# The last pair of a state-space block: decays and gates recorded ahead of the previous pair's outputs

## The chip, the core and the metric

The kernel runs on one core of a Trainium2 chip, in one launch. The metric is the time of the launch on the device in microseconds (us), the median of several runs; lower is better. Five engines of the core work side by side, each through its own queue in the order of that queue: TensorE (PE in the profile, with its weight loads as PEld), VectorE (DVE), ScalarE (ACT), GpSimd (POOL) and SyncE (SP), which here only issues DMAs. They wait for each other by semaphores.

## The reference

Two pre-norm layers act on x, 4 sequences of 256 positions with 512 features. Cut to its frame:

```python
x = x + attn0(layernorm(x))    # 1: gated linear attention, 32 heads, chunks of 128
x = x + ffn0(layernorm(x))     # 2: top-8 router over 64 experts, a bias mix
x = x + attn1(layernorm(x))    # 3: state space: conv, decays, gate, group norm, out_proj
x = x + ffn1(layernorm(x))     # 4: top-16 of 64 low-rank adapters
```

The change is in block 3, the state space, as it hands over to block 4. What block 3 computes for one head, with chunks of 128 positions:

```python
hs, B, C = split(silu(conv4(x @ W_x)))           # causal convolution of 4 taps
L        = exp(segsum(dt * A))                   # the decays, 128 x 128, lower triangle
Y        = (C @ B.T * L) @ (hs * dt) + off_chunk + D * hs
g        = Y * silu(x @ W_gate)
out      = rmsnorm_by_group(g) * norm_w @ W_out
```

Block 4 takes a layernorm of the result, scores 64 adapters, keeps 16, softmaxes them into gates, and computes `((x @ A) * gates) @ B`.

## The kernel before

**Tiling.** x stays on the chip as eight tiles of 128 positions by 512 features (`k.x[0..7]`). Tiles 0 to 3 are half 0 (sequences 0 and 1), tiles 4 to 7 half 1. The normalized input of a half is held transposed, split into two parts `xs_hi` and `xs_lo`. Each weight is split likewise by `split` (L138 on ACT makes the high part, L141 on POOL the low part), and each product is three matmuls of 128x512: high by high, low by high, high by low. A projection (`proj`, L200) is 12 such matmuls.

**Block 3** goes by pairs of 128-channel tiles: 8 groups, 4 pairs in a group, 2 halves, so 64 pairs, in the list `pairs`. The last four are, as (group, pair, half): (7,2,0), (7,3,0), (7,2,1), (7,3,1). I write U for (7,3,0), the last pair of half 0; V for (7,2,1); and Z for (7,3,1), the last pair of all. Every pair goes through these steps, each named by a letter; a digit is the channel tile (0, 1) or, for O, the output tile (0 to 3):

- I `inputs`: projection ps_x, then the convolution (L712 on ACT, three times L714 on DVE) and Silu (L1115 on ACT).
- X `sums`: a DMA brings running sums into gb, and m is formed from them (L293 on DVE and POOL, L295 on POOL).
- D `decays`: two Exp on ACT (L1115), then m times C.B, 128x1536, on DVE (L753).
- G `gate`: projection ps_g, then Silu on ACT.
- T `turn`: four transposes into ps_t (L775), then xd (L777) and xe (L786) on DVE. xe lies in the buffer with the tag "xn", of which there is one; the normalization of block 4 takes the same buffer for its first and fourth tile.
- M `mixer`: 24 small matmuls into ps_y (L800); then xs on DVE (L810), times the gate on POOL (L814), yh on ACT (L818), yl on DVE (L819); the square on ACT (L826) and its sum on POOL (L828).
- O `output`: six matmuls into ps_o (L854), added to acc on DVE (L860). At the last pair of a group also the scale r (L834 on PE, L839 on DVE, L840 on POOL), and L863 on DVE adds the scaled acc to the four x tiles of the half.
- B, the shared projection of a group, does nothing for the last pair. W splits one more weight, if one is due.
- P and E `pump`: one step of side work from `k.side`. E may also run a step that needs another activation table.

**Staging.** One round i of the loop in `run` takes three neighbouring pairs: O is of `before` (pair i-1), T and M are of `p` (pair i), and I, G, X, D are of `after` (pair i+1). The order inside a round is a string of letters, written out by hand: STEP3, or SIDE3 if `k.side` is not empty as the round begins. PSUM has eight banks by tags of two: "x", "y", "o" and "g"; ps_o has the tag "o", so a ps_o waits until the acc step two outputs before it has been done.

The scheduler keeps the recorded order as a priority and may move instructions of one engine past each other.

**Handing over.** When O3 of U is recorded, half 0 is ready, and `prepare4(0)` of block 4 goes into `k.side`. Its steps: wr (the router weight, put into the tag "xd" and then split: L962 on ACT, L963 on POOL, into the buffer that acc of half 0 leaves); the moments (L86, L88 on DVE, rstd by L90 and L91 on POOL) and the first centred tiles xn (L99); four steps of transposes ps_xn (L107) with the parts xs_hi (L124, ACT) and xs_lo (L125, DVE); the scores ps_lg; their top 16 on DVE (L976 to L996); then eight projections ps_h; in their course the gates are transposed (L999), copied (L1001) and sent by DMA to DRAM and back, spread (L1047). The same for half 1 follows when O3 of Z is recorded. Block 4 proper multiplies ps_h by the gates (L1056), splits it (L1061, L1062) and multiplies by B (L1077).

The round that the change touches is the one with p = V, before = U, after = Z. In the kernel before, `k.side` is empty as it begins, so its order is STEP3. The rounds after it use SIDE3.

Of the kernel before, what the change touches and what calls it, by code (L numbers as in the profile page):

```python
# [18 lines left out]
P = 128  # L19
# [13 lines left out]
STEP1 = "K S0 W T S1 S2 W G0 G1 K C K P U A0 K W P A1 T P P Q0 N0 W W N1 Q1 T T W K D F".split()  # L33
SIDE1 = "S0 W G0 T P K C W W P P W S1 K G1 S2 U P A0 N0 A1 P Q0 T W T F W N1 K Q1 T T D W W".split()
STEP3 = "W T0 T1 B I0 W M0 M1 X0 X1 I1 O0 G0 W W O1 W W P O2 W W G1 P W O3 D0 D1 W W".split()
SIDE3 = "T0 T1 I0 I1 M0 M1 P B X0 X1 P P O0 W O1 G0 G1 W W P O2 O3 W P W P D0 D1 E E".split()


# [615 lines left out]
def state_space(k, tc, io):  # L654
# [65 lines left out]
    def group(p):  # L720

        g, half = p.g, p.half
        bc = [
            k.wk.tile([P, FREE], F32, tag="y", name=f"bc_{g}_{half}_{n}", bufs=4) for n in range(2)
        ]
        for n, first in enumerate((BS, CS)):
            conv(proj(k, tc, chunk(p.w.bc(), n), half, f"bc_{g}_{half}_{n}"), bc[n], first + g)
        s = own.only.tile([P, 3, 2, P], F32, tag="cb", name=f"cb_{g}_{half}", bufs=2)
        for b in range(2):
            ps = k.psum.tile([P, 3, P], F32, tag="x", name=f"ps_cb_{g}_{half}_{b}")  # L730
            for n, (zs, zl) in enumerate(((0, 0), (1, 1), (0, 1))):
                fs, fl = (2 * b + zs) * P, (2 * b + zl) * P
                nc.tensor.matmul(
                    ps[:, n, :], bc[0][:, fs:fs + P], bc[1][:, fl:fl + P],
                    start=True, stop=True,
                )
            nc.scalar.copy(s[:, :, b, :], ps)
        cbs[g, half] = s

    def sums(p, n):  # L740
        hs = slice(2 * (p.ch + n), 2 * (p.ch + n) + 2)
        p.e[n] = exponents(
            k, tc, cum[p.half][:, hs, :], start[p.half][:, :, hs], f"{p.name}_{n}", 2
        )

    def decays(p, n):


        m, across = p.e.pop(n)
        k.act(m[:, 2], across, AF.Exp)  # L750
        k.act(m[:, 0:2], m[:, 0:2], AF.Exp)
        mh = m.rearrange("p z (h b) l -> p z h (b l)", h=2)
        made = nc.vector.tensor_tensor(  # L753
            mh, mh, cbs[p.g, p.half].rearrange("p z b l -> p z (b l)").unsqueeze(2)
            .to_broadcast([P, 3, 2, 2 * P]), ALU.mult,
        )
        p.m.append(m)
        p.due.append(made)

    def inputs(p, n):  # L760
        xs = k.wk.tile([P, FREE], F32, tag="a", name=f"xs_{p.name}_{n}", bufs=4)
        conv(proj(k, tc, chunk(p.w.x(), n), p.half, f"x_{p.name}_{n}"), xs, p.ch + n)
        p.xs.append(xs)

    def gate(p, n):
        sg = k.wk.tile([P, FREE], F32, tag="sg", name=f"sg_{p.name}_{n}", bufs=4)
        k.act(sg, proj(k, tc, chunk(p.w.g(), n), p.half, f"g_{p.name}_{n}", "g"), AF.Silu)
        p.sg.append(sg)

    def turn(p, n):  # L770

        nm, ch, xs = f"{p.name}_{n}", p.ch + n, p.xs[n]
        ps = k.psum.tile([P, HT, P], F32, tag="y", name=f"ps_t_{nm}")
        for t in range(HT):
            nc.tensor.transpose(ps[:, t, :], xs[:, t * P:t * P + P], k.ident)  # L775
        xd = k.wk.tile([P, HT, 2, D], F32, tag="xd", name=f"xd_{nm}")
        made = nc.vector.tensor_tensor(  # L777
            xd, ps.rearrange("p t (h d) -> p t h d", h=2),
            dt[p.half][:, :, 2 * ch:2 * ch + 2].unsqueeze(3)
            .to_broadcast([P, HT, 2, D]), ALU.mult,  # L780
        )
        p.xd.append(xd)
        p.due.append(made)
        if n == 0:
            p.xe = k.wk.tile([P, 2, 2, 2, D], F32, tag="xn", name=f"xe_{p.name}", bufs=1)
        made = nc.vector.tensor_tensor(  # L786
            p.xe[:, n], ps.rearrange("p (b z) (h d) -> p b z h d", b=2, h=2)[:, :, 0],
            start[p.half][:, 2, 2 * ch:2 * ch + 2, :].rearrange("p h b -> p b h").unsqueeze(3)
            .to_broadcast([P, 2, 2, D]), ALU.mult,
        )  # L790
        p.due.append(made)
# [50 lines left out]
    def output(p, t):  # L842
        if p.cp == 0 and t == 0:
            acc[p.g, p.half] = k.wk.tile([P, HT, HID], F32, tag="big", name=f"acc_{p.name}")
        if p.cp == NC // 2 - 1 and t == 0:
            scale(p)
        ps = k.psum.tile([P, HID], F32, tag="o", name=f"ps_o3_{p.name}_{t}")
        at = slice(t * P, t * P + P)
        i = 0
        for n in range(2):  # L850
            yh, yl = p.y[n]
            wh, wl = p.w.o()
            for y, w in ((yh, wh), (yh, wl), (yl, wh)):
                nc.tensor.matmul(ps, y[:, at], w[:, n, :], start=(i == 0), stop=(i == 5))  # L854
                i += 1
        a = acc[p.g, p.half][:, t, :]
        if p.cp == 0:
            nc.scalar.copy(a, ps)
        else:
            nc.vector.tensor_tensor(a, a, ps, ALU.add)  # L860
        if p.cp == NC // 2 - 1:
            xt = k.x[HT * p.half + t]
            nc.vector.scalar_tensor_tensor(xt, a, p.r[:, t:t + 1], xt, ALU.mult, ALU.add)  # L863
# [3 lines left out]
    pairs = []  # L867
# [21 lines left out]
    def run(done):  # L889


        with tc.tile_pool(name="s3", bufs=1, reuse_waits="tile") as own.only:
            for i in range(-1, len(pairs) + 1):
                k.bank = BANK3
                before, p, after = (
                    pairs[j] if 0 <= j < len(pairs) else None for j in (i - 1, i, i + 1)
                )
                if i + 2 < len(pairs):
                    k.weights.due = pairs[i + 2].w.g.n
                else:  # L900
                    k.weights.due = len(k.weights.all) - 1
                if after is not None and after.half not in ready:
                    k.pump(1000, True)

                def shared():
                    if after.cp == 0:
                        group(after)

                def put(t):
                    output(before, t)  # L910
                    if t == HT - 1 and all(one.half != before.half for one in pairs[i:]):
                        done(before.half)

                step = dict(
                    B=shared, I=lambda n: inputs(after, n), G=lambda n: gate(after, n),
                    X=lambda n: sums(after, n), D=lambda n: decays(after, n), T=lambda n: turn(p, n), M=lambda n: mixer(p, n),
                    O=put, W=k.weights.step, P=k.pump, E=lambda: k.pump(1, True),
                )
                for one in SIDE3 if k.side else STEP3:
                    who = {"T": p, "M": p, "O": before, "P": k, "E": k, "W": k}.get(one[0], after)  # L920
                    if who is not None and (i >= 0 or not AHEAD or one[0] not in "IG"):
                        step[one[0]](*(int(n) for n in one[1:]))
# [325 lines left out]
```

## Time and profile before

| what | value |
|---|---|
| median of 3 runs | 2592.67 us (2592.57 to 2594.05) |
| the profiled execution, time | 2597.62 us |
| the profiled execution, span of the core | 2595.9 us |
| mean granted TensorE clock | 0.983 |
| PE busy | 2468.8 us, 95% |
| DVE busy | 2082.8 us, 80% |
| ACT busy | 1531.7 us, 59% |
| POOL busy | 1528.2 us, 59% |
| DMA | 206.18 MB, mean 79 GB/s |

The profile is of one execution; its span and its time differ by 1.7 us of launch, and its time is 4.95 us above the median. "PE 128*128 128x512" is a matmul with a 128x128 weight over 512 columns. In a timeline a row has the start, the duration, the engine, the line and what it writes and reads; brackets give the idle time before it and what ended it. In a table of windows, PEclk is the clock that TensorE was granted in that stretch, 1.00 being full speed. Places in the trace are given in us from the start of the span.

### The profile page before, as it was taken

The page shows a single profiled execution, that of the slowest core. Times are in us where ns is not written, and L with a number is a line of the kernel's source. Part 1 is how long each engine was busy: PE and PEld are TensorE (multiplying, and loading weights), DVE is VectorE, ACT ScalarE, POOL GpSimd, SP SyncE. Part 2 cuts the span into 40 slices and gives each one's busy share as a digit, 9 for nine tenths or more (in the row PEclk, how much of TensorE's full clock was granted, in tenths as well). Part 3 has the DMA queues.
Part 4 walks back from the last instruction along what each step waited for, and adds up shares of the span by engine and source line. Part 5 has one row for each costly group of instructions (what it writes and reads, how often), then busy time and mean ns, then how long its engine had stood idle before and what let it go on. Part 6 is the DMA issues. An engine that isn't in the chain of part 4 may idle for free.

```text
span 2595.9 us, 35580 instructions
## 1 busy us (share of the span) xinstructions
PE 2468.8 (95%) x13488; PEld 1998.4 (77%) x13488; DVE 2082.8 (80%) x2694; ACT 1531.7 (59%) x2109; POOL 1528.2 (59%) x996
## 2 busy tenths in 40 slices
PE   7899999999999888989999999999999999999889
PEld 6777787888777676768878788788787887887667
DVE  6777777778888767797997888888888888879963
ACT  3665565666665545565765756666656657657531
POOL 4554445456655545586774864856766756747840
PEclk9999999999999988999999999999999999999989
DMA  3321111212221222242322222322323223323321
GB/s 106 82 66 49 54 52 57 66 57 90 90 86 56 86 73 69 80 120 74 98 90 66 84 88 82 98 73 78 102 65 98 82 74 93 96 63 100 94 73 67
DMA packets 82891, 206.18 MB, mean 79 GB/s; under 512 B 8672, under 2 KB 10592, under 8 KB 82720
## 3 DMA queue, kind: packets, MB, share of 16 engines
q1 hardware_dynamic: 82720, 203.90, 25.8%
q8 instruction: 107, 1.75, 0.3%
q14 instruction: 64, 0.52, 0.1%
HBM read 200.86 MB, written 3.01 MB: 79 GB/s over the span
## 4 chain that ended last, share of the span: by engine, by line
PE 59%; DVE 25%; ACT 5%; POOL 5%; issue 4%; DMA 2%; SPq 0%; POOLq 0%; ACTq 0%; DVEq 0%
PE ps_g L200 12%; PE ps_o L854 8%; PE ps_x L200 6%; PE ps_o L458 6%; PE ps_q L200 6%; DVE conv L714 5%; DVE m L753 5%; PE ps_y L800 3%; PE ps_y L411 3%; PE ps_sc L399 2%; DVE x L863 2%; PE ps_bc L200 2%; DVE m L293 2%; PE ps_h L200 2%; PE ps_o L1077 2%
## 5 line engine op out<-in xcount | busy, mean ns | idle before, releaser
L200 PE MATMUL ps_g<-xs_hi,wg_h 128*128 128x512 f32 x768 | 309.2, 403 | 18.5 <-ACT wg_h L138 7.3
L200 PE MATMUL ps_g<-xs_lo,wg_h 128*128 128x512 f32 x768 | 305.5, 398 | 0.0
L200 PE MATMUL ps_g<-xs_hi,wg_l 128*128 128x512 f32 x768 | 304.1, 397 | 1.1 <-POOL wg_l L141 1.1
L753 DVE TENSOR_TENSOR m<-m,cb 128x1536 f32<-128x1536 f32 x128 | 264.9, 2081 | 47.5 <-ACT m L1115 43.2
L714 DVE SCALAR_TENSOR_TENSOR conv<-ps_x,cw,conv 128x510 f32<-128x510 f32 (+2 forms) x384 | 270.7, 737 | 17.7 <-ACT conv L712 14.4
L1112 ACT ACT_TABLE_LOAD x193 | 247.6, 1283 | 3.9 <-PEq L1236 0.8
L141 POOL TENSOR_TENSOR wo_l<-raw_wo,wo_h 128x1024 fp32r<-128x1024 f32 x60 | 154.8, 2580 | 136.1 <-ACT wo_h L138 136.1
L1115 ACT ACTIVATE xs<-conv,cb 128x512 f32<-128x512 f32 x128 | 91.6, 723 | 239.9 <-DVE conv L714 236.8
L293 POOL TENSOR_TENSOR m<-gb,start 128x512 f32<-128x512 f32 x128 | 152.4, 1194 | 136.1 <-PE ps_y L800 107.8
L814 POOL TENSOR_TENSOR xs<-xs,sg 128x512 f32<-128x512 f32 x128 | 201.2, 1572 | 43.1 <-DVE xs L810 42.5
L854 PE MATMUL ps_o<-wo_h,yh 128*128 128x512 f32 x512 | 213.0, 416 | 9.8 <-DVE acc L860 6.9
L295 POOL TENSOR_SCALAR_AFFINE_SELECT m<-m 128x1024 f32<-128x1024 f32 x160 | 216.0, 1350 | 1.5 <-DVE m L293 1.4
L200 PE MATMUL ps_x<-xs_hi,wx_h 128*128 128x512 f32 x512 | 206.4, 403 | 7.8 <-DVE conv L714 7.8
L854 PE MATMUL ps_o<-wo_h,yl 128*128 128x512 f32 x512 | 200.5, 402 | 6.4 <-DVE yl L819 6.3
L200 PE MATMUL ps_x<-xs_lo,wx_h 128*128 128x512 f32 x512 | 204.9, 400 | 0.0
L200 PE MATMUL ps_x<-xs_hi,wx_l 128*128 128x512 f32 x512 | 203.6, 398 | 0.0
L854 PE MATMUL ps_o<-wo_l,yh 128*128 128x512 f32 x512 | 203.1, 397 | 0.0
L828 POOL TENSOR_TENSOR sqs<-sqs,sq 128x512 f32<-128x512 f32 x112 | 173.0, 1545 | 48.6 <-ACT sq L826 48.1
L141 POOL TENSOR_TENSOR wx_l<-raw_wx,wx_h 128x1024 fp32r<-128x1024 f32 x38 | 97.7, 2571 | 176.1 <-DVE conv L714 115.8
L141 POOL TENSOR_TENSOR wg_l<-raw_wg,wg_h 128x1024 fp32r<-128x1024 f32 x60 | 158.9, 2648 | 61.0 <-ACT wg_h L138 58.9
L200 PEld LDWEIGHTS ps_g<-xs_hi,wg_h 128*128 128x128 f32 x768 | 144.8, 189 | 61.0 <-issue 17.1
L800 PE MATMUL ps_y<-m,xd 128*64 128x128 f32 x2048 | 177.2, 279 | 14.3 <-DVE m L753 13.6
(281 smaller groups left out, 6963.9 us busy)
## 6 DMA issues: line engine op xcount, KB each, us to landing
gb<-cum SPq DMA_DIRECT2D x160, 512.0 KB
raw_wx<-in_L_attn_in_x_dram SPq DMA_DIRECT2D x38, 512.0 KB
raw_wg<-in_L_attn_in_gate_dram SPq DMA_DIRECT2D x38, 512.0 KB
raw_wo<-n_L_attn_out_proj_w_dram SPq DMA_DIRECT2D x38, 512.0 KB
raw_wq<-in_L_attn_Wq_dram SPq DMA_DIRECT2D x22, 512.0 KB
raw_wg<-in_L_attn_Wg_dram SPq DMA_DIRECT2D x22, 512.0 KB
raw_wo<-in_L_attn_Wo_dram SPq DMA_DIRECT2D x22, 512.0 KB
raw_wkv<-in_L_kv_dram SPq DMA_DIRECT2D x11, 512.0 KB
```

The source lines that it names most:

```text
L141: nc.gpsimd.tensor_tensor(lo, w, hi.bitcast(F32), ALU.subtract)
L200: tc.nc.tensor.matmul(ps, a[:, c, :], b[:, c, :], start=(c == 0 and n == 0), stop=(c == KC - 1 and n == 2))
L293: engine.tensor_tensor(m[:, blk], gb[:, min(blk, 1)], last(at, P), ALU.add)
L295: nc.gpsimd.affine_select(out=causal, in_=causal, compare_op=ALU.is_ge, fill=GONE, base=0, pattern=[[0, 8], [1, P]], channel_multiplier=-1,)
L458: nc.tensor.matmul(ps, y[:, 2 * h + b, :], w[:, h, :], start=(i == 0), stop=(i == 5))
L714: nc.vector.scalar_tensor_tensor(acc[:, :, j:], ps[:, :, :SEQ - j], cw[:, ch, TAPS - 1 - j:TAPS - j], acc[:, :, j:], ALU.mult, ALU.add,)
L753: made = nc.vector.tensor_tensor(mh, mh, cbs[p.g, p.half].rearrange("p z b l -> p z (b l)").unsqueeze(2) .to_broadcast([P, 3, 2, 2 * P]), ...
L800: one = nc.tensor.matmul(ps_y[h * D:h * D + D, 2 * b + z, :], p.xe[:, n, b, h, :] if blk == 2 else xd[:, 2 * b + zs, h, :], m[:, blk, 2 * ...
L814: nc.gpsimd.tensor_tensor(xs, xs, p.sg[n], ALU.mult)
L828: nc.gpsimd.tensor_tensor(total, total, sq, ALU.add)
L854: nc.tensor.matmul(ps, y[:, at], w[:, n, :], start=(i == 0), stop=(i == 5))
L1112: load = nc.scalar.preload_act_table_set(table)
```

## The change

For the one round whose `after` is the last pair, a third order is used:

```diff
 STEP3 = "W T0 T1 B I0 W M0 M1 X0 X1 I1 O0 G0 W W O1 W W P O2 W W G1 P W O3 D0 D1 W W".split()
+LAST3 = "T0 T1 I0 I1 X0 X1 M0 M1 G0 G1 W D0 D1 W O0 O1 P W O2 O3 P W P P E P E".split()
 SIDE3 = "T0 T1 I0 I1 M0 M1 P B X0 X1 P P O0 W O1 G0 G1 W W P O2 O3 W P W P D0 D1 E E".split()
...
-                for one in SIDE3 if k.side else STEP3:
+                for one in LAST3 if after is pairs[-1] else SIDE3 if k.side else STEP3:
```

Against STEP3, both gates of Z (G0, G1) and both decays of Z (D0, D1, with the products of L753) are recorded ahead of all four outputs of U. I1 is recorded ahead of M0, as are X0 and X1. Behind O3, where STEP3 has D0 D1, there are six pumps: wr, the moments and the four transposes of half 0 of block 4 are thus recorded in this round, ahead of T, M and the outputs of the next one, which were ahead of them. There are four W in place of eleven. No instruction is added or removed in number on DVE, ACT, POOL, SP or PE.

## The prediction, made before the changed kernel had run

> **What bounds the kernel now.** I read the page first, for the engine that sets the time:
>
> ```profile
> PE 2468.8 (95%) x13488; PEld 1998.4 (77%) x13488; DVE 2082.8 (80%) x2694; ACT 1531.7 (59%) x2109; POOL 1528.2 (59%) x996
> PEclk9999999999999988999999999999999999999989
> PE 59%; DVE 25%; ACT 5%; POOL 5%; issue 4%; DMA 2%; SPq 0%; POOLq 0%; ACTq 0%; DVEq 0%
> ```
>
> The first line is busy time, the last the chain that ended last. PE is busy for 95% of the span, so nothing is won but where PE waits or is slowed; one of the few slices below 9 in PEclk is the last but one. So I read the table of windows from where the change begins to the end (columns: window, length, PE, PEld, DVE, ACT, POOL busy, PEclk, DMA share, GB/s):
>
> ```profile
> 2436.00:2456.00 20.00, 18.00 (x122) 14.57 (x120) 17.39 (x25) 11.17 (x16) 18.34 (x12) 1.00 0.26 79
> 2456.00:2470.00 14.00, 5.24 (x51) 4.07 (x50) 14.00 (x16) 2.44 (x3) 10.87 (x9) 0.76 0.29 86
> 2470.00:2485.00 15.00, 13.34 (x55) 9.95 (x55) 13.37 (x19) 7.34 (x12) 14.87 (x12) 0.89 0.27 76
> 2485.00:2512.00 27.00, 27.00 (x128) 21.73 (x127) 13.07 (x49) 7.95 (x13) 9.10 (x11) 1.00 0.14 41
> 2512.00:2526.00 14.00, 9.27 (x30) 6.73 (x29) 7.06 (x11) 4.54 (x9) 0.00 (x0) 0.63 0.35 105
> 2526.00:2592.00 66.00, 66.00 (x292) 53.56 (x290) 27.47 (x62) 9.79 (x16) 2.39 (x1) 1.00 0.21 72
> ```
>
> There are two weak places: 2452 to 2474, and 2512 to 2526. From 2526 PE is never idle, so a gain ahead of it reaches the end whole. In the first place DVE is busy for 14.00 of 14: it is the engine to follow there. Then the timeline of PE, the rows with idle time:
>
> ```profile
> 2455.04 0.50 PE L854 MATMUL ps_o<-wo_h,yh 128*128 128x512 f32 x1 [2.00 <-ACT yh L818]
> 2461.68 0.69 PE L800 MATMUL ps_y<-m,xd 128*64 128x128 f32 x4 [5.46 <-DVE m L753]
> 2465.51 0.44 PE L800 MATMUL ps_y<-m,xd 128*64 128x128 f32 x4 [1.01 <-DVE m L753]
> 2470.44 0.66 PE L107 MATMUL ps_xn<-ident,xn 128*128 128x128 f32 x4 [2.74 <-DVE xn L99]
> 2514.04 0.66 PE L107 MATMUL ps_xn<-ident,xn 128*128 128x128 f32 x4 [1.02 <-DVE xs_lo L125]
> 2517.30 0.76 PE L200 MATMUL ps_lg<-xs_hi,wr_parts 128*128 128x512 f32 x1 [2.60 <-DVE xs_lo L125]
> 2520.89 0.80 PE L200 MATMUL ps_lg<-xs_lo,wr_parts 128*128 128x512 f32 x1 [1.12 <-DVE xs_lo L125]
> ```
>
> With two small gaps (0.54, 0.67) PE waits for 17.2 us. It also runs at half clock: matmuls follow each other at 0.43 us instead of 0.23 after several of these gaps. Priced by the number of matmuls, that loses 1.4 us at 2461.7, 1.9 at 2470.4 to 2474.4 and 3.9 at 2514 to 2525.7, in all 7.2. So 24.4 us are lost here, 15.8 in the first place and 8.6 in the second (4.74 idle, 3.9 clock). More than 24 us cannot be won.
>
> **The change part by part.** In number nothing is added on any engine; all of the change is order. The built queues are the same up to the end of ps_y of V, 2439.65 us. From there PE does g of Z (24 matmuls), the rest of o_U0 and o_U1, ps_t of Z, o_U2 and o_U3, all of o_V, the four ps_xn of half 0, and only then ps_y of Z, the scores, and the ps_h with o_Z between them. Before, ps_y of Z stood ahead of every ps_xn.
>
> Part 1, gates and decays earlier. The g of Z end at 2445.3 by 0.23 us a matmul, so ACT has the last Silu at 2448.3 (2449.4 before), and after one table load (1.28) and its Exps at 2452.6 the second m (2454.3 before). DVE can run the two L753 at 2451.1 and 2454.7 instead of 2457.98 and 2462.06, ahead of the four L863, instead of behind. I take 3.0 us for each:
>
> ```profile
> L753 DVE TENSOR_TENSOR m<-m,cb x6: 2119/3006/3842, 2408.5 to 2462.1; 128x1536 f32<-128x1536 f32 x6
> ```
>
> (duration: shortest, median, longest.) The wait of 5.46 us for m thus goes, and m is early by 20 us where it is now used. But the two products now stand ahead of what PE needs: acc of o_U2, whose PSUM bank the o of V wait for, and yl of V. PE waits 0.85 us for r ahead of ps_t (behind yl of V, at 2449.0), 2.3 for acc behind the first product (to 2454.7), 2.7 for yl behind the second (to 2458.6), then 1.2 in two waits for acc. PE is through o_V at 2466.5.
>
> Part 2, six pumps early. The four L863 (mean 0.87, so 3.5 us) end at 2463.3. ACT's L962 follows them, as wr's parts take acc's buffer, and behind it in ACT's queue two casts of wa (1.04 each). On POOL L963 and two L141 (2.4 each) are queued ahead of the three L91 that give rstd: 2465.2, 2467.6, adds 2468.2, 2470.6, and rstd at 2471.2. In the kernel before, two of the three L91 were done at 2468.9. The first xn is ready at 2471.8: PE waits 5.3 us for it, where it waited 2.74. This is the new wait, and it takes the place of the old 5.46. In the chain xn, ps_xn, xs_hi, xs_lo three more gaps follow, 1.2, 1.6 and 0.8: xs_hi of the second tile is queued on ACT behind a cast of raw_wb, whose DMA leaves after the second L141, and the fourth xn shares its buffer with xe. ps_y of Z begins at 2478.1. The DMA of wr passes ahead of three raw_wa on SP; those wa are used 10 us later, so I cost that at nothing, and 1.0 us (one cast, as above) if that cover fails.
>
> The sum of gaps is 0.85 + 2.3 + 2.7 + 1.2 + 5.3 + 1.2 + 1.6 + 0.8 = 15.95 us. For the half clock I take one loss of 1.9 (as at 2470.4) after 2.7, one after 5.3, and 1.5 in the short gaps behind it: 5.3. The first place thus costs 21.2 instead of 15.8: worse by 5.4.
>
> [...] The row: after 2.00 us of idle (2455.04) the matmuls still came at 0.23, after 2.74 (2470.44) at 0.43. [...]
>
> Part 3, the end. The outputs of Z now stand between the ps_h, which are work for PE while the top 16 of half 0 are found. The gates leave earlier: L999 at 2502.9 instead of 2508.3, gT at 2503.5 instead of 2509.6, and with the 6.25 us from gT to the first L1056 and 1.85 from one to the next, as before, the first gates come at 2509.8 and 2511.65. So half 1 is normalized with 12 o-matmuls beside it and PE waits 1.1 us in place of 4.74, at full clock: 7.5 of the 8.6 are won.
>
> Sum: 5.4 - 7.5 = **-2.1 us**. The profiled run took 2597.62, 4.95 above the median; the same difference from the median gives 2590.6.
>
> The bounds of what is unknown: both L753 at 2.12, -1.8; no half clock after 2.7, -1.9; no gap in the tail, -1.1; yl at its median 0.92 instead of 1.65, -0.7: together -7.6. Upwards: L753 at 3.84, +1.7; one L141 at 3.87 (as at 2459.88), +1.5; half clock for another four us behind the 5.3, +1.9: together +3.0. I take the middle values, because DVE and POOL are as full here as in the rows they come from.
>
> **The rivals.** *Cheap middle, faster.* The low ends come together: DVE is ahead, as the decays no longer collide with the moments. For it speaks that L753 has a mean of 2.08 over the whole kernel; against it, that POOL is busy for 18.34 of 20 us where the products now go, and the products on either side took 3.84 and 3.56. At -7.6: 2585.1; if the 2.3 gap and the loss of clock after the 5.3 go too, -11.8, 2580.9.
>
> *Late gates, slower.* In the new queue of DVE the first L1056, which waits for a DMA, is ahead of the last moments and xn of half 1, and on ACT the hid_h of the second gate is ahead of the copy that empties a PSUM bank for ps_h. By my times that copy ends at 2513.6 and PE needs the bank at 2514.1: 0.5 us of room. From a gT later than 2504 on, PE waits, the clock falls, and the 8.6 of the tail stay. For it speaks that gT hangs on L996, whose chain the first place delays; against it, that o_Z gives PE 48 matmuls (11 us) to bridge. At 5.4 + 0 to + 1.7 (L753 at 3.84): between +5.4 and +7.1, 2599.0; with 1.0 for the cast as well, 2600.8.
>
> That the change moves nothing is excluded by the built queues.
>
> **How the numbers follow.** Forecast .46, cheap middle .30, late gates .24. A measurement of this kernel can tell about 0.2%, 5.2 us, from no change. The forecast's own range, 2585.1 to 2595.7, is mostly within that: .32 same, .12 faster, .02 slower. The cheap middle is .30 faster; late gates .23 slower, .01 same. Faster .42, same .33, slower .25. The range runs from 2581 to 2600.
>
> **What would show it.** In the timeline of PE: no wait for m L753 ahead of ps_y; a wait of about 5 us for xn L99, 2.3 and 2.7 us ahead of L854; PEclk of 1.00 from 2512 on. On DVE both L753 ahead of the L863. gT earlier by 6 us. It is wrong if the ps_xn are not late, or if ps_h waits for a raw4 copy behind L1061.

## The result, and the profile after

The changed kernel is slower: 2600.55 us against 2594.41 us (medians of 22 runs each), a ratio of 1.0022 with an interval of 1.0015 to 1.0030, which is 5.7 us (3.9 to 7.8). A second comparison gave 1.0014 (1.0005 to 1.0023). The kernel before, compared with itself in the same way, gave 1.0005 (0.9995 to 1.0014): differences under 0.1% are not read as differences below. The forecast was -2.1 us.

The page of the changed kernel (profiled run 2600.39 us, span 2598.7 us):

```profile
PE 2471.4 (95%) x13488; PEld 1999.9 (77%) x13488; DVE 2081.2 (80%) x2694; ACT 1530.7 (59%) x2109; POOL 1530.3 (59%) x996
PEclk9999999999999988999999999999999999999889
PE 60%; DVE 24%; ACT 6%; POOL 4%; issue 4%; DMA 2%; SPq 0%; POOLq 0%; ACTq 0%; DVEq 0%
```

PE has 2.6 us more busy time with the same number of matmuls, and one slice more of PEclk, the last but two, is below 9: the clock, not only the idle time, is part of the loss. (Lines of the kernel are one higher than before: L753 is L754, L863 is L864, L854 is L855.) The table of windows, with the columns as before:

```profile
2436.00:2456.00 20.00, 15.76 (x104) 12.46 (x100) 18.14 (x20) 11.87 (x16) 20.00 (x13) 0.98 0.24 76
2456.00:2470.00 14.00, 8.92 (x19) 5.87 (x19) 13.38 (x19) 2.52 (x3) 9.90 (x8) 0.54 0.30 83
2470.00:2485.00 15.00, 8.98 (x67) 7.13 (x68) 6.18 (x11) 4.36 (x8) 8.36 (x8) 0.66 0.31 100
2485.00:2512.00 27.00, 27.00 (x127) 21.78 (x128) 16.80 (x52) 7.79 (x13) 10.93 (x12) 1.00 0.15 45
2512.00:2526.00 14.00, 11.53 (x55) 8.61 (x53) 9.43 (x16) 5.78 (x11) 2.02 (x3) 1.00 0.24 86
2526.00:2592.00 66.00, 64.71 (x280) 52.69 (x281) 27.34 (x63) 9.96 (x16) 2.39 (x1) 0.97 0.19 68
```

The window to 2526 was repaired (PEclk 0.63 before, 1.00 now), as forecast. But part of the loss moved behind it: from 2526 on, where PE was never idle before, it now idles for 1.3 us and the clock is 0.97. The second and third windows were made worse: 0.54 and 0.66 where they had 0.76 and 0.89. The timeline of PE, the rows with idle time:

```profile
2447.92 0.63 PE L776 MATMUL ps_t<-ident,xs 128*128 128x128 f32 x4 [1.07 <-DVE r L840]
2453.57 0.47 PE L855 MATMUL ps_o<-wo_h,yh 128*128 128x512 f32 x1 [2.13 <-ACT wo_h L139]
2456.82 0.79 PE L855 MATMUL ps_o<-wo_h,yl 128*128 128x512 f32 x1 [1.85 <-DVE yl L820]
2463.61 0.80 PE L855 MATMUL ps_o<-wo_h,yh 128*128 128x512 f32 x1 [3.27 <-DVE acc L861]
2473.69 1.97 PE L108 MATMUL ps_xn<-ident,xn 128*128 128x128 f32 x8 [4.68 <-DVE xn L100]
2476.31 1.09 PE L108 MATMUL ps_xn<-ident,xn 128*128 128x128 f32 x4 [0.65 <-DVE xs_lo L126]
2478.47 1.12 PE L108 MATMUL ps_xn<-ident,xn 128*128 128x128 f32 x4 [1.07 <-DVE xs_lo L126]
2480.19 0.69 PE L801 MATMUL ps_y<-m,xd 128*64 128x128 f32 x4 [0.61 <-DVE xe L787]
2515.88 0.50 PE L201 MATMUL ps_h<-xs_hi,wa_h 128*128 128x512 f32 x1 [0.51 <-ACT raw L1014]
2521.05 0.50 PE L1078 MATMUL ps_o<-wb_2h,hid_l 128*128 128x512 f32 x1 [0.31 <-DVE hid_l L1063]
2527.29 0.79 PE L201 MATMUL ps_lg<-xs_lo,wr_parts 128*128 128x512 f32 x1 [2.94 <-DVE xs_lo L126]
```

The 5.46 us for m are gone. In their place the idle time lies in eight pieces ahead of ps_y of Z, and a new one of 2.94 us ahead of ps_lg of half 1.

To compare traces I use the stretch from the start of the last row of ps_y of V (2439.33 before, 2437.72 after) to the end of the span; what lies ahead of it is the same work in both. It is 156.6 us before and 161.0 after. Its loss has three shares: PE's idle time in the first 46 us of the stretch (about up to the scores of half 0), its idle time after that up to the last matmul, and the time lost at half clock. This last is an estimate: half of PE's busy time in the intervals whose granted clock is 0.50, as matmuls follow each other at 0.43 us there and at 0.23 elsewhere.

| kernel | ratio to before (interval) | stretch | idle, first 46 us | idle, rest | half clock |
|---|---|---|---|---|---|
| before | | 156.6 | 12.4 | 4.7 | 6.8 (3.1 in the first 46) |
| before_again | 1.0005 (0.9995 to 1.0014) | 154.8 | 12.4 | 3.7 | 5.8 (3.1) |
| after | 1.0022 (1.0015 to 1.0030) | 161.0 | 15.3 | 3.8 | 9.0 (7.5) |
| after_again | 1.0014 (1.0005 to 1.0023) | 158.0 | 15.2 | 2.4 | 7.5 (7.5) |
| no_pumps | 1.0022 (1.0013 to 1.0030) | 161.7 | 12.7 | 6.7 | 8.4 |
| pumps_only | 0.9993 (0.9984 to 1.0002) | 154.3 | 15.8 | 1.9 | 4.1 |
| gates_early | 1.0020 (1.0011 to 1.0029) | 158.8 | 15.0 | 2.4 | 8.5 |
| decays_early | 1.0012 (1.0000 to 1.0024) | 156.7 | 14.8 | 2.6 | 6.6 |
| one_pump | 1.0006 (0.9997 to 1.0015) | 158.6 | 12.9 | 2.0 | 10.9 |
| gate_swap | 1.0005 (0.9996 to 1.0015) | 157.3 | 14.6 | 0.9 | 9.0 |
| rstd_first | 1.0004 (0.9993 to 1.0015) | 157.3 | 12.8 | 3.3 | 8.8 |
| pool_quiet | 1.0001 (0.9992 to 1.0009) | 155.6 | 13.4 | 3.5 | 5.3 |
| pool_quiet_swap | 0.9994 (0.9984 to 1.0004) | 154.3 | 13.6 | 1.9 | 5.8 |
| products_late | 1.0005 (0.9994 to 1.0015) | 157.2 | 14.8 | 2.6 | 7.5 |
| quiet_pumps | 0.9993 (0.9982 to 1.0004) | 152.0 | 11.8 | 2.6 | 5.2 |
| quiet_late | 0.9993 (0.9982 to 1.0004) | 151.5 | 13.2 | 0.9 | 5.3 |
| products_mid | 0.9990 (0.9981 to 0.9999) | 152.9 | 13.0 | 1.6 | 6.0 |
| products_last | 0.9995 (0.9987 to 1.0004) | 155.3 | 10.6 | 5.5 | 7.4 |
| products_last_loud | 1.0004 (0.9994 to 1.0014) | 156.9 | 12.6 | 4.1 | 8.4 |
| warm | 1.0018 (1.0008 to 1.0027) | 160.4 | 12.6 | 2.5 | 8.7 (7.0) |

After against before, in the two first traces: +2.9 idle in the first 46 us, +4.5 at half clock there, -1.0 idle later, -2.3 at half clock later, together about 4.1 of the 4.4 us by which the stretch grew.

### The profile page after: what moved, and what is told of

Same layout as the page of the kernel before. It is cut to its first block, busy times and chain, and to the rows that moved or that the text cites. A ratio compares the mean times of both kernels' runs of the same rounds, so it can differ in the third digit from the quotient of the medians.

```text
span 2598.7 us, 35582 instructions
## 1 busy us (share of the span) xinstructions
PE 2471.4 (95%) x13488; PEld 1999.9 (77%) x13488; DVE 2081.2 (80%) x2694; ACT 1530.7 (59%) x2109; POOL 1530.3 (59%) x996
## 3 DMA queue, kind: packets, MB, share of 16 engines
q8 instruction: 107, 1.75, 0.3%
## 4 chain that ended last, share of the span: by engine, by line
PE 60%; DVE 24%; ACT 6%; POOL 4%; issue 4%; DMA 2%; SPq 0%; POOLq 0%; ACTq 0%; DVEq 0%
PE ps_g L201 12%; PE ps_o L855 8%; PE ps_x L201 6%; PE ps_o L459 6%; PE ps_q L201 6%; DVE conv L715 5%; DVE m L754 4%; PE ps_y L801 4%; PE ps_y L412 3%; PE ps_sc L400 2%; PE ps_bc L201 2%; DVE m L294 2%; DVE x L864 2%; DVE yl L820 2%; PE ps_v L201 2%
## 5 line engine op out<-in xcount | busy, mean ns | idle before, releaser
L754 DVE TENSOR_TENSOR m<-m,cb 128x1536 f32<-128x1536 f32 x128 | 261.7, 2057 | 46.6 <-ACT m L1116 42.3
L715 DVE SCALAR_TENSOR_TENSOR conv<-ps_x,cw,conv 128x510 f32<-128x510 f32 (+2 forms) x384 | 270.7, 737 | 17.6 <-ACT conv L713 14.3
L855 PE MATMUL ps_o<-wo_h,yh 128*128 128x512 f32 x512 | 213.7, 418 | 12.6 <-DVE acc L861 9.5
L855 PE MATMUL ps_o<-wo_h,yl 128*128 128x512 f32 x512 | 202.0, 404 | 8.2 <-DVE yl L820 8.1
L855 PE MATMUL ps_o<-wo_l,yh 128*128 128x512 f32 x512 | 204.3, 399 | 0.0
L820 DVE SCALAR_TENSOR_TENSOR yl<-xs,nw,yh 128x512 fp32r<-128x512 f32 x128 | 157.3, 1229 | 39.6 <-ACT yh L819 39.5
```

The costliest lines, as they stand in the source:

```text
L715: nc.vector.scalar_tensor_tensor(acc[:, :, j:], ps[:, :, :SEQ - j], cw[:, ch, TAPS - 1 - j:TAPS - j], acc[:, :, j:], ALU.mult, ALU.add,)
L754: made = nc.vector.tensor_tensor(mh, mh, cbs[p.g, p.half].rearrange("p z b l -> p z (b l)").unsqueeze(2) .to_broadcast([P, 3, 2, 2 * P]), ...
L820: nc.vector.scalar_tensor_tensor(yl, xs, w, yh.bitcast(F32), ALU.mult, ALU.subtract)
```

## The experiments

A call `k.behind(a, b, reason)` in the diffs fixes that a follows b in the queue of their engine, as the kernel itself does for its table loads; `k.mark` holds instructions by name.

### Which half of the change costs

**no_pumps**: the early letters without the pumps.

```diff
-LAST3 = "... G0 G1 W D0 D1 W O0 O1 P W O2 O3 P W P P E P E".split()
+LAST3 = "... G0 G1 W D0 D1 W O0 O1 W O2 O3 W".split()
```

> The third order without its six pumps behind O3; gates and decays of Z stay early. Theory 1 (the pumps cost: they put the ps_xn, and the casts and moments ahead of them, in front of ps_y of Z): the 4.7 us wait for xn ahead of ps_y of Z is gone, ps_y of Z follows the second L753 directly, and the time is that of before or up to 3 us less. Theory 2 (the early products cost: two L753 ahead of acc and the scaled x): the waits of 1.9 and 3.3 us ahead of L855 stay and the time is that of after, +5 us or more against before.

Measured: 1.0022, as slow as the change. Theory 2 holds. ps_y of Z now comes after a wait of 1.55 us for m, but the outputs of V wait 3.69 us for yl and 3.80 for acc behind the products and the scaled x, and the scores of half 0 come later and wait 2.64 us for xs_lo. Of the 6.7 us of idle time in the column of the rest, 3.7 lie around those scores and 3.0 in the tail.

**pumps_only**: the pumps without the early letters.

```diff
+LAST3 = STEP3 + "P P P E P E".split()
```

> The order of before as it was, with nothing but the six pumps added at its end; gates and decays of Z are recorded behind the outputs of U, as before. The built queues of PE, DVE, ACT and POOL are those of after, row for row, two rows differ on SP. Theory 1 (of the edited string only the pumps reach the chip, the early letters D and G change nothing once the pumps are there): the time of after, +5 to 6 us against before, with both L753 ahead of the scaled x all the same. Theory 2 (the recorded order matters beyond the queues): the time of before.

The premise of this expectation, that the queues are those of after, was wrong: in the trace the g of Z are mixed with the outputs of U, and the scaled x stand ahead of both products. So it is what its name says, and it measured 0.9993: neither theory as I had put it, but a clear split of the change. Its rows in the timeline of PE:

```profile
2457.71 0.50 PE L855 MATMUL ps_o<-wo_h,yh 128*128 128x512 f32 x1 [2.00 <-ACT yh L819]
2466.55 1.22 PE L855 MATMUL ps_o<-wo_h,yl 128*128 128x512 f32 x2 [7.65 <-DVE yl L820]
```

The idle time in the first 46 us is no less than in after (15.8), but half of it is one wait of 7.65 us. The loss at half clock is 4.1 us in place of 9.0.

**gates_early** and **decays_early** add one pair of early letters each to pumps_only.

```diff
-... X1 I1 O0 G0 W W O1 W W P O2 W W G1 P W O3 D0 D1 W W P P P E P E
+... X1 I1 G0 G1 O0 W W O1 W W P O2 W W P W O3 D0 D1 W W P P P E P E   (gates_early)
+... X1 I1 D0 D1 O0 G0 W W O1 W W P O2 W W G1 P W O3 W W P P P E P E   (decays_early)
```

> The order of before with the six pumps at its end and both gates of Z moved ahead of the outputs of U; the decays stay behind the last output of U. Theory 1 (the early gates cost: 24 matmuls and the Silus go ahead of the outputs of U, r and the scaled x come later and meet the splits of POOL): the time of after, 5 us against before, 6 to 7 us against the kernel with the pumps only. Theory 2 (the early decays cost): the time of the kernel with the pumps only, 0.999 to 1.000.

> The order of before with the six pumps at its end and both decays of Z moved ahead of the outputs of U; the gates stay among the outputs. Theory 1 (the early gates cost): the time of the kernel with the pumps only, within 3 us of before, with the g matmuls mixed with the outputs of U. Theory 2 (the early decays cost): the two L754 stand ahead of acc and of the scaled x on DVE, 5 us slower than before.

Measured: 1.0020 and 1.0012 (1.0000 to 1.0024). Theory 1 holds for the gates: G0 G1 ahead of the outputs bring nearly all of the loss against pumps_only, and their trace shows the waits of after ahead of ps_xn (4.68, 0.65, 1.07) even though D0 D1 were recorded last: once the gates were early, the products were put ahead of the scaled x in the queue all the same. DVE in gates_early, then in pumps_only:

```profile
2449.78 2.32 DVE L754 TENSOR_TENSOR m<-m,cb 128x1536 f32<-128x1536 f32 x1 [0.76 <-ACT m L1116]
2452.62 2.23 DVE L754 TENSOR_TENSOR m<-m,cb 128x1536 f32<-128x1536 f32 x1
2456.03 7.00 DVE L864 SCALAR_TENSOR_TENSOR x<-acc,r,x 128x512 f32<-128x512 f32 x3
```

```profile
2456.60 2.74 DVE L864 SCALAR_TENSOR_TENSOR x<-acc,r,x 128x512 f32<-128x512 f32 x4 [1.83 <-POOL r L841]
2459.26 1.75 DVE L754 TENSOR_TENSOR m<-m,cb 128x1536 f32<-128x1536 f32 x1
2462.71 2.12 DVE L754 TENSOR_TENSOR m<-m,cb 128x1536 f32<-128x1536 f32 x1
```

The early gates also put 24 matmuls ahead of the outputs of U on PE; no run parts that from the new order on DVE. The stretch of gates_early is 4.5 us longer than that of pumps_only, with 0.3 us less idle time in all and 4.4 us more lost at half clock.

decays_early settles less than it seems to. Its interval holds what either theory forecast, and it moved more than the decays: with the Exps ahead of the gates' Silus, ACT loads its tables 195 times in all, 193 in every other kernel here, and the cast of wo_h comes behind the added loads (1.28 us each). PE waits 5.17 us for it, where after has 2.13. What early decays cost by themselves stays open.

**one_pump**: after with one pump behind O3 in place of six.

```diff
-... O2 O3 P W P P E P E
+... O2 O3 P W
```

> After with one pump behind O3 (wr) in place of six. In the built queue of PE ps_y of Z then goes ahead of every ps_xn again, with wr and the products still early. Theory 1 (what costs is that ps_y of Z, ready 20 us early, stands behind the late xn): ps_y of Z fills 3 us of the 4.7 us wait, its own half clock stays, the time is 2 to 3 us less than after, +3 against before. Theory 2 (the early products in front of acc and of the scaled x cost): the waits of 1.9 and 3.3 us stay and the gain is taken back by xn: the time of after.

Measured: 1.0006, a stretch 2.3 us shorter than that of after and 0.6 longer than that of after_again. ps_y of Z fills part of the wait for xn (1.49 and 1.32 remain of 4.68), but the waits of 1.84 and 3.27 us stay and the half clock takes 10.9 us. By the ratio it is theory 1, by the stretch it is not settled.

### What stands ahead of what

**gate_swap**: one pair of instructions of DVE swapped in after.

```diff
         second()
+        k.pump(5, True)
...
-                nc.vector.tensor_tensor(gate, gate, ps, ALU.mult)
+                made = nc.vector.tensor_tensor(gate, gate, ps, ALU.mult)
+                if half == 0 and c in (2,):
+                    k.behind(made, k.mark["lo_4_7"], "gate late")
```

> After with one pair of DVE instructions swapped: the last xs_lo of half 1 goes ahead of the one gate multiply that waited until 2525.94 for its DMA. Theory 1 (that multiply, and nothing else, holds ps_lg): the wait of 2.94 us ahead of ps_lg and about 1.7 us of half clock behind it go, 4.6 us less than after, +1 us against before. Theory 2 (the gates are late in themselves): PE waits for the same DMA a little later, ahead of L1079, and the time is that of after, +5 to 6 us against before.

Measured: 1.0005; theory 1. The timeline of DVE after the swap:

```profile
2522.95 1.28 DVE L126 TENSOR_TENSOR xs_lo<-ps_xn,xs_hi 128x512 fp32r<-128x512 f32 x2
2525.37 0.69 DVE L1058 TENSOR_TENSOR gate<-gate,raw 128x512 f32<-128x512 f32 x1 [1.14 <-DMA gate<-gates]
```

In after the multiply, waiting for its DMA until 2525.94, stood between those two xs_lo. Its wait now holds nobody, and ps_lg of half 1 has no wait in the timeline. In the trace the swap is the only difference on DVE, and ACT and POOL have the order of after. So the tail's new wait was one multiply in the wrong place.

**rstd_first**: the low part of wa_6 behind the third pow.

```diff
-LAST3 = "... O2 O3 P W P P E P E".split()
+LAST3 = "... O2 O3 P P W P E P E".split()
...
-    nc.gpsimd.tensor_tensor(lo, w, hi.bitcast(F32), ALU.subtract)
+    low = nc.gpsimd.tensor_tensor(lo, w, hi.bitcast(F32), ALU.subtract)
+    if name in ('wa_6',):
+        k.behind(low, k.mark["pow_4_2"], "split late")
```

> After with one split of a weight of block 4 (the low part of wa_6 on POOL, 2.3 us) put behind the three pow of rstd instead of ahead of them. Theory 1 (the queue of POOL holds xn): the wait ahead of the first ps_xn falls from 4.7 to 2.3 us, 2.4 us less than after, +3.3 against before. Theory 2 (xn is late because DVE is late with the scaled x and the moments): the wait stays over 4 us and the time is that of after.

Measured: 1.0004. The wait for xn falls from 4.68 to 1.30 us and the idle time in front by 2.6, so POOL's queue held xn. But ps_xn then waits 2.43 us for xs_lo, and PE waits 3.25 us for hid_h in the tail: it is earlier than the gates' DMAs. Other instructions of DVE, ACT and POOL changed places with the split, so the ratio is not the price of this one alone.

**pool_quiet**: four splits behind the pow, so that POOL is empty while DVE scales x; **pool_quiet_swap** adds the edit of gate_swap.

```diff
-LAST3 = "... G0 G1 W D0 D1 W O0 O1 P W O2 O3 P W P P E P E".split()
+LAST3 = "... G0 G1 D0 D1 O0 O1 O2 O3 P P W W W W P E P E".split()
...
+    if name in ('wo_7_3_1', 'wa_2', 'wa_4', 'wa_6'):
+        k.behind(low, k.mark["pow_4_2"], "split late")
```

> After with four splits of weights (low parts of wo of Z, wa_2, wa_4, wa_6 on POOL) put behind the three pow of rstd. POOL then does nothing from the second sum of squares of V to the low part of wr. Theory 1 (POOL's splits slow DVE beside them and queue ahead of rstd): L864 takes 0.7 to 0.8 us each in place of 1.9, the wait of 3.3 us for acc goes, the wait of 4.7 for xn falls under 2.5, and the end is 5 us or more ahead of after, level with before or better. Theory 2 (DVE is slow by itself there, and the splits must be paid somewhere): L864 stays near 1.9, or the splits delay xs of Z and PE waits there, and the time is that of after.

> The kernel with the quiet POOL and the swap of the last xs_lo and the gate multiply together. If both repairs count by themselves (theory 1), 3.5 us less than the quiet POOL alone, 3 to 5 us ahead of before (0.9982 to 0.999). If the gates' DMAs are the next bound in the tail (theory 2, the wait for hid_h of 3.25 us that the kernel with rstd first showed), the swap brings nothing more than the quiet POOL alone and the time is within 2 us of before.

Measured: 1.0001 and 0.9994. First the answer for the line of the scaled x in after, from 2450 to 2465 (the durations are shortest, median and longest, in ns), then the same for pool_quiet:

```profile
L864 DVE SCALAR_TENSOR_TENSOR x<-acc,r,x x4: 735/1494/2835, 2457.3 to 2463.5; 128x512 f32<-128x512 f32 x4
```

```profile
L866 DVE SCALAR_TENSOR_TENSOR x<-acc,r,x x4: 740/740/743, 2457.3 to 2459.9; 128x512 f32<-128x512 f32 x4
```

They begin at the same place, and each takes 0.74 us without a split beside it, up to 2.84 with one; the split itself takes 2.8. The last x begins 3.6 us earlier. The wait of 3.27 us for acc is gone, the first xn waits 1.39. The splits are paid for in part where they went: the xn ahead of them took 0.53 us, the two behind it 2.50 and 2.47, and PE then waits 2.36 for the second. Theory 1 for the four x, with a bill. The swap on top brings 0.7 of a thousandth, less than can be told.

**products_late**: the pumps and the order of before, with both L754 of Z behind the third xn.

```diff
+LAST3 = "... O3 W W P P D0 D1 P E P E".split()
...
+        if p is pairs[-1]:
+            k.behind(made, k.mark["xn_4_2"], "last products late")
```

> The order of before with the six pumps, and both products L753 of Z put behind the third xn of half 0 on DVE. Theory 1 (the early products hold acc, yl and the scaled x, and POOL beside them makes them slow): the waits of 1.9 and 3.3 us ahead of L855 go with about 3 us of half clock, xn comes 4 us earlier, and the end is 7 us ahead of after, 1 us ahead of before. Theory 2 (something has to be late: ps_y of Z now waits for the products): a wait of 5 us for m ahead of ps_y of Z takes their place and the time is that of after.

Measured: 1.0005, no better than pumps_only. The wait for yl falls from 7.65 to 3.24 us, but ps_xn waits 5.90 for xs_lo behind the two products: theory 2 in substance, though the wait is for xs_lo and not for m.

### Whether the traces and the cause hold

**after_again** is the changed kernel and **before_again** the kernel before, both unedited.

> The changed kernel once more, unchanged. Theory 1 (the waits are set by the queues): the same waits within 0.3 us in the timeline of PE (2.1 for wo_h, 1.9 for yl, 3.3 for acc, 4.7 for xn, 2.9 for xs_lo ahead of ps_lg) and 1.002 against before. Theory 2 (they are of one execution): waits that differ by over 1 us, and a time nearer to that of before.

> The kernel before once more. Theory 1: its stretch from the last ps_y of V to the end is within 2 us of the first trace's 156.3 us, and its idle time in front of ps_lg near 12.4 us. Theory 2 (the stretch varies from one execution to the next as much as the kernels differ): 153 or 160 us.

The waits of after in front of ps_y of Z come again within 0.12 us (2.14, 1.85, 3.26, 4.68, 0.65, 0.95, 0.61). The one ahead of ps_lg is 1.60 in place of 2.94: it hangs on a DMA and belongs partly to the execution, and this time the clock did not fall behind it. So theory 1 holds but for this one wait, and that makes 3 us of difference between two executions of one kernel. before_again has 12.4 us of idle time in front, as before, and a stretch 1.8 us shorter.

**warm**: after with 36 transposes that do no work of the kernel, written into the bank of the first ps_xn and overwritten.

```diff
+    for n in range(warm):
+        for c in range(KC):
+            tc.nc.tensor.transpose(ps[:, c, :], k.x[3][:, c * P:(c + 1) * P], k.ident)
...
+        ps = turned(k, tc, xn, f"xn_{tag}_{t}", 9 if (tag, t) == ("4", 0) else 0)
```

> After with 36 transposes of 128x128 of the fourth x tile added ahead of the first ps_xn, into the bank that it writes, which it then overwrites: PE has 4 us of work in its wait of 4.7 us for xn. Theory 1 (the half clock is what the spread waits cost): the idle time falls to about 1 us there, the clock is full from the ps_xn on, the loss at half clock in front of ps_lg falls from 7.5 to 4 or 5 us, and the time is 2 to 3 us less than after although PE has more to do. Theory 2 (DVE and POOL set the pace and the clock follows): the time of after, or up to 2 us more, as the added transposes delay the real ones.

Measured: 1.0018, as after. The wait for xn is gone, but the added transposes came ahead of the last output of V and ran at half clock themselves at first (5.65 us for 36: the first 6 came at 0.21 us, the last 16 at 0.11), and ps_xn waited 3.67 us for xs_lo instead, behind which the clock fell once more. ps_y of Z starts 42.8 us into the stretch, in after 42.5. This is theory 2, with a reservation: the loss at half clock in front was 7.0 us, so the run doesn't show what an undisturbed clock would have brought. The low part of wa_6 also stands behind the pow in this kernel's trace, as in rstd_first.

### Towards a better version

**quiet_pumps** and **quiet_late** join the quiet POOL and the swap with the pumps and the order of before; in quiet_late both products stand behind the third xn.

```diff
+LAST3 = "... I1 O0 G0 O1 O2 G1 O3 D0 D1 P P W W W W W P E P E".split()   (quiet_pumps)
+LAST3 = "... I1 O0 G0 O1 O2 G1 O3 P P D0 D1 W W W W W P E P E".split()   (quiet_late)
```

> The kernel with the pumps only, with the four splits of POOL behind the three pow of rstd and the last xs_lo of half 1 ahead of the gate multiply. Theory 1 (a split on POOL and an operation of DVE that reads two operands from SBUF hold each other up for their full length, and the pumps by themselves gain): the wait of 7.7 us for yl falls to 4 or less, the one for xn to 2, and the time is 5 to 8 us less than before, 0.997 to 0.998. Theory 2 (DVE's own work bounds the stretch): the waits move to xs_lo and xe, and the time is that of the pumps only, 0.999.

> As the kernel with quiet POOL, the pumps and the swap, and with both L754 of Z behind the third xn on DVE. Theory 1 (yl of V and the moments go first, nothing stands ahead of the first xn): PE waits 2 us for yh and at most 2 for xn, then 4 to 5 us for xs_lo behind the two products; 5 to 8 us less than before. Theory 2 (the products must be paid ahead of ps_y of Z wherever they are put): the time of the kernel with quiet POOL and pumps, within 2 us.

**products_mid**, **products_last** and **products_last_loud** put the products behind the second, or behind the last xs_lo of half 0; the loud one has neither quiet POOL nor swap.

```diff
+LAST3 = "... I1 O0 G0 O1 O2 G1 O3 P P P P D0 D1 W W W W W P E".split()    (products_mid)
+LAST3 = "... I1 O0 G0 O1 O2 G1 O3 P P P P P P D0 D1 W W W W W".split()    (products_last)
+LAST3 = "... O3 W W P P P P P P D0 D1".split()    (products_last_loud, the rest as STEP3)
...
+        k.behind(made, k.mark["lo_4_1"], "last products late")    (products_mid)
+        k.behind(made, k.mark["lo_4_3"], "last products late")    (products_last, _loud)
```

> Quiet POOL, the pumps, both L754 of Z behind the second xs_lo of half 0, so that two of the four xs_lo and xe of Z stand behind the products. Theory 1 (order): between quiet_late and products_last, a wait of 4 to 5 us for xs_lo or xe ahead of ps_y of Z, 0.997 to 0.999. Theory 2: no difference between the three.

> Quiet POOL, the pumps, and both L754 of Z behind the last xs_lo of half 0. In the built queue of PE the scores and 17 matmuls of ps_h go ahead of ps_y of Z. Theory 1 (order bounds the stretch): the wait of 7 us for xs_lo behind the two products (quiet_late) is gone, PE does the scores and ps_h while DVE multiplies, and the time is 8 to 10 us less than before, 0.996 to 0.997. Theory 2 (DVE's total work bounds it): PE waits as long for m ahead of ps_y of Z, or for yl of Z ahead of the outputs, or for the gates in the tail, 0.999 as the kernels with quiet POOL.

> The same without the quiet POOL and without the swap: the pumps, the order of before, both L754 of Z behind the last xs_lo of half 0. Theory 1 (order): 4 us less than the pumps only, 0.997 to 0.998; the splits of POOL cost 2 to 3 us against the quiet kernel of the same order. Theory 2: as the pumps only, 0.999.

Measured, in the order of the names above: 0.9993, 0.9993, 0.9990, 0.9995 and 1.0004. By the time, theory 2 holds for the four quiet ones: in quiet_pumps yl is still waited for 5.91 us, in quiet_late xs_lo 7.04. The loud one came out above both of its theories; against the quiet kernel of the same order (0.9995) it lost 2.3 us, which the intervals do not tell from nothing. The four quiet ones beat the changed kernel by 5 to 8 us; against before they gain 1 to 3 us where I had expected 5 to 10. products_last has the least idle time in front (10.6), but then waits 4.80 us for xn of half 1 in the tail: what ps_y of Z loses in place comes back behind it, as theory 2 said. products_mid is the best; its interval (0.9981 to 0.9999) just leaves out 1, and with a control of 1.0005 I would not call it faster than before on this evidence.

## Why the prediction was wrong, step by step

**What held.** PE's order, the end of the wait for m, both L753 ahead of the scaled x, the wait for xn (5.3 expected, 4.68 measured), for r (0.85 and 1.07), ahead of the first output of V (2.3 and 2.13) and for yl (2.7 and 1.85). The sum of gaps in front was 15.95 in the prediction and is 15.33 (15.2 again). That the first place would get worse was in it too. The 2.13 us were forecast as a wait for acc; the profile ends them with the cast of wo_h, and both ended together:

```profile
2452.42 1.03 ACT L139 CAST wo_h<-raw_wo 128x1024 fp32r<-128x1024 f32 x1
2452.76 0.67 DVE L861 TENSOR_TENSOR acc<-acc,ps_o 128x512 f32<-128x512 f32 x1
```

So the cast, which the prediction did not name, would have held PE as long without acc.

**Where the miss lies.** The first place was to cost 5.4 us more and cost 7.4 more in the first traces (7.2 in the second ones); the tail was to win 7.5 and won 3.2 (4.0). So the larger part of the miss is step 3 below, then step 2. Step 1 is wrong in its price, but the idle time in front came out right in sum.

**Step 1 that failed, the price of the scaled x.** Part 1 took 1.2 us for the waits for acc behind them, at 0.87 us for each L863. Measured, the wait is 3.27 us, and the four take 2.25, 2.84, 0.74 and 0.74. The 0.87 is the mean of the last eight in the trace of before: seven took 0.74 to 0.75 with no split beside them, one 1.77 beside a sum of squares on POOL. The mean of all 64 there is 1.39. In the rows of after the two slow ones begin at 2457.29 and 2459.46, and each ends 0.55 us after the split that was running when it began:

```profile
2456.18 2.81 POOL L142 TENSOR_TENSOR wo_l<-raw_wo,wo_h 128x1024 fp32r<-128x1024 f32 x1
2458.95 2.79 POOL L142 TENSOR_TENSOR wa_l<-raw_wa,wa_h 128x1024 fp32r<-128x1024 f32 x1
```

pool_quiet shows the other side of it: with no split beside them all four took 0.74. By what means a split lengthens an operation of DVE is not shown. In the sum this miss was hidden by waits that were shorter than forecast: for yl by 0.85 us (the products took 2.88 and 1.74, not 3.0 each), for xn by 0.6, and the three behind it by 1.3.

**Step 2 that failed, the half clock.** Part 2 took 5.3 us in the first place; it is 7.5 in both traces of after. I had read one row, "no fall after 2.00 us of idle", as a rule for single gaps. Single gaps do not tell the falls in after: behind the wait of 2.13 us the matmuls came at 0.23 us (from 2453.88), behind the shorter one of 1.85 at 0.43 (from 2458.01). Here is the table of windows of after, cut into windows of 3.41 us, on whose edges the granted clock changes in this trace (same columns):

```profile
2448.28:2451.70 3.42, 3.16 (x15) 2.21 (x13) 3.04 (x4) 3.41 (x6) 3.42 (x3) 1.00 0.22 43
2451.70:2455.11 3.41, 1.40 (x5) 0.86 (x5) 3.41 (x4) 2.80 (x4) 3.41 (x2) 1.00 0.28 111
2455.11:2458.52 3.41, 1.70 (x4) 1.20 (x5) 3.41 (x3) 0.00 (x0) 3.41 (x2) 0.50 0.02 5
2458.52:2461.94 3.42, 1.83 (x5) 0.91 (x3) 3.42 (x2) 0.00 (x0) 3.22 (x2) 0.50 0.49 150
2461.94:2465.35 3.41, 1.74 (x4) 1.45 (x5) 3.41 (x7) 1.10 (x2) 0.40 (x1) 0.50 0.53 160
2465.35:2468.76 3.41, 3.41 (x9) 2.31 (x8) 3.25 (x9) 0.47 (x1) 3.41 (x4) 0.50 0.00 0
2468.76:2472.18 3.42, 0.24 (x1) 0.00 (x0) 0.78 (x2) 1.04 (x1) 2.35 (x4) 1.00 0.53 153
```

The first figure behind the length is PE's busy time. A window in which PE was busy for 1.40, 1.70, 1.83 or 1.74 us is followed by one at 0.50, a window of 3.16 or 3.41 by one at 1.00. So PE, about half busy in four windows on end with the outputs of V in three pieces, did 19 of their 24 matmuls at half clock. In pumps_only, with its one long wait, the same windows look like this:

```profile
2456.69:2460.10 3.41, 1.19 (x4) 0.67 (x4) 3.41 (x5) 3.41 (x6) 1.42 (x1) 1.00 0.16 64
2460.10:2463.51 3.41, 0.00 (x0) 0.00 (x0) 3.41 (x5) 0.48 (x1) 3.41 (x2) 0.50 0.00 0
2463.51:2466.93 3.42, 0.38 (x1) 0.38 (x2) 3.42 (x6) 0.06 (x1) 3.42 (x2) 0.50 0.51 156
2466.93:2470.34 3.41, 3.06 (x7) 1.94 (x7) 2.08 (x5) 0.99 (x1) 3.41 (x5) 0.50 0.13 24
2470.34:2473.75 3.41, 1.83 (x8) 1.12 (x6) 1.88 (x4) 1.04 (x1) 3.41 (x5) 1.00 0.34 130
```

Two windows with almost no work cost themselves and the half clock of one busy window behind them. That is most of the difference between after and pumps_only: 17.7 us idle there, 19.1 and 17.6 in the two traces of after, but 4.1 us lost at half clock against 9.0 and 7.5. That the half clock is also the cause of those microseconds, and not a companion of DVE's pace, is argued from this arithmetic and not shown; the run that should have shown it (warm) did not.

**Step 3 that failed, the tail.** 1.1 us of idle time and no half clock were forecast, 3.76 and 1.5 came (2.4 and none in the second trace). gT was ready at 2504.6, with the 1.6 us by which after's stretch begins earlier that is 2.7 later than forecast, and the first multiply by the gates took 2.71 us beside a split on POOL. The rival of the late gates had the mechanism, a gate multiply that waits for its DMA in DVE's queue, but not the place: it stood ahead of the last xs_lo. gate_swap shows its price: 3.7 us of the stretch against the first trace of after, 0.7 against the second, and 0.9 to 1.7 thousandths by the ratios, 2 to 4 us; against after_again the intervals overlap. The sign that the prediction had named against itself, a ps_h that waits for a raw copy behind the gates' casts, is in the trace as well, with 0.51 us. The forecast saw the multiply ahead of the moments and of xn, gave it half a microsecond of room, and did not look at what stood behind the later ones.

The rival's sum, +5.4 to +7.1, held the measured 5.7, but by luck and not by its own shares: it had +5.4 in the first place and nothing won in the tail, and the two first traces have +7.4 and -3.2. The cheap middle, which took 2.12 for each L753, was near with them (1.74 and 2.88 here, 1.75 and 2.12 in pumps_only) and was wrong all the same, as DVE was not ahead for it.

**What the prediction did not ask** is which of the moved letters does the work. It priced the decays and the pumps; the gates were only a date (2445.3). With the six pumps they are enough for the loss: 1.0020 with them, 0.9993 without. They are not the whole cause: one_pump has them too and measured 1.0006. Four different repairs of after, each by itself, brought it to between 1.0001 and 1.0006 (one_pump, gate_swap, rstd_first, pool_quiet), and their gains add up to far more than the loss of 1.4 to 2.2 thousandths. So by these ratios they overlap, and how the loss divides among the waits stays open.

## What to carry to other kernels

Price an operation from a row that has the same neighbour on the other engine: here a scaled x of 0.74 us on DVE took up to 2.84 beside a split of 2.8 on POOL. Where PE must wait anyway, look at how its work lies in the windows on whose edges the clock was seen to change (3.41 us here) and not only at the idle time: in these traces 17.7 us of idle time with one long wait lost 4.1 us at half clock, 17.6 us spread between the matmuls 7.5. And in a queue kept in order, look at every instruction that waits for a DMA and at who stands behind it; one swap was worth 2 to 4 us of a loss of 4 to 6 by the ratios, the lower end not clear of the noise.

## What the runs showed of the hardware that was not expected

In the traces of before and after every stretch at one granted clock, but for the last, which the end of the trace cuts, is a whole multiple of 3.41 us. What followed a window of that length went with the clock that it had as well as with PE's work in it: 1.83 us of 3.41 was followed by 0.50 in after, where the window itself had 0.50, and by 1.00 in pumps_only, where it had 1.00. In the traces of before and after, from 2430 to 2560 us, 61 windows had full clock: the 6 that were followed by half clock held 0.24 to 1.51 us of PE work, the others at least 2.31. Of 14 windows at half clock, the 6 that were followed by full clock held at least 2.70 us, the others at most 2.3. So here a half-busy window could keep the full clock (1.83 in pumps_only) but did not win it back. The point is not one number for all work: earlier in the trace of before a window at full clock with 2.21 us of PE work (from 764.55) was followed by half clock and one with 1.53 (from 884.01) by full clock, and two at half clock with 3.41 (from 989.83) were followed by half clock. In after the window ahead of the first fall (from 2451.70) was not empty: it held 1.40 us of matmuls.

An xn (128x512, one operand and two columns) took 0.54 us in after with POOL idle beside it (2514.61), and 2.18 in before (2470.91) beside a split of 2.38: an operation with one large operand took longer too. And r, a tile of 128x4, took 2.53 us on POOL in after beside an L754 of 2.88, 1.02 in before: here it is the operation of POOL that took longer.
